# Second scores of the first group in shared PSUM banks, beside the next unit's first scores

## Chip, cores and metric

The kernel runs on one core of a Trainium2 chip. The metric is the device time of one execution in microseconds (us), as a median of several runs. The engines that matter are TensorE (PE in the profile, with its weight loads as PEld), VectorE (DVE), ScalarE (ACT), GpSimd (POOL) and SyncE (SP), which issues most transfers. They run their own instruction streams in order and wait for one another by semaphores.

## What is computed

A batch of 16 sequences of 100 tokens with 256 features goes through cross-attention on 361 context tokens (16 heads of 16 features), and then through a soft mixture of experts: 16 experts with 64 slots each. Both are residual.

```python
q, k, v = norm(x) @ wq + bq, ctx @ wk + bk, ctx @ wv + bv      # 16 heads of 16
alpha   = softmax(q k^T / 4 + mask)                            # over 361 keys
x       = x + (alpha v) @ wo + bo
xn      = layernorm(norm(x));  se = layernorm(slot_embeds) * scale
logits  = xn se^T                                              # 100 tokens, 1024 slots
slots   = softmax(logits over tokens)^T xn
eout    = (gelu(slots Wg + bg) * (slots Wu + bu)) Wd + bd      # per expert
x       = x + softmax(logits over slots) eout
```

Everything is in fp32.

## The kernel before

**Groups and units.** The 16 sequences are worked in groups of 2, 2, 4, 4 and 4 (`GROUPS`). A group's attention is cut into *units*: one sequence `b` and one block `cb` of four heads. The first group has 8 units. After a group's attention its logits and slots are made (`dispatch_quarter`), and then the stream of experts (`experts`, `down`, `combine_quarter`) runs over it, while units of the next group are laid between. Once the experts have begun there is always work for PE.

**A unit** (class `Unit`) has four steps:
- `maxima`: four products of 32 rows each (one per head, in the four 32-row strips of the array) put the *first scores*, tokens by keys, into the four PSUM banks of the tile `at` (L785); VectorE takes their negated maxima over the keys into `mxp` (L790).
- `queries`: PE transposes the maxima (L799, into a free corner of bank 0 of `at`), and VectorE adds them to the queries (L801), in a row that was kept free. The second scores so come out with the maximum taken off.
- `exponentials`: twelve products, three blocks of keys by four heads, put the *second scores*, keys by tokens, over the same four banks (L810); one ScalarE instruction takes the exponentials of all four, 121 by 1200 (L818).
- `values`: twelve products with the values (L833) give the unnormalised context and the sums; ScalarE copies them out (L842).

Since `at` serves both scores, a unit's first scores stand behind the exponentials of the unit before (`free_t`). The values of the last unit are taken after the first scores of the present one. Everything else on PE uses four further banks in turn (`mm_tile`).

**Beside the units** lie generators in the list `fill`: `key_work` (context transposes L584, keys L613, values L673, mask rows by DMA from SP L653), `query_work` (L519, L538), `parameter_work` (L405), `bo_work` (L423), `slot_work` (statistics of the slot embeddings L436, a power on GpSimd L447, their deviation L460, normalising them on ScalarE L467, transposing them L476 and L482) and `out_work` (reciprocal of the sums L713 and L714, output product L726, normalising the tokens L747, their transpose L752 and L758).

**What sets the order.** The kernel is written out in Python by a small planner: `Clock` keeps a modelled time for each engine and each bank, each generator yields the time at which its next step could go, how many banks it needs and the time that it needs on PE, VectorE and ScalarE, and the loop at the end takes the first task whose time has come. The modelled times only decide the order; on the chip the order stands and each instruction waits for what it needs. Until the experts begin (`begun`), a side task is only taken where it *fits* ahead of the next step of the unit, and where nothing fits the planner places a *warm* product: identity by identity, which nobody reads, into the last columns of bank 3 of `at` (L1344).

Of the kernel before, what the change touches and what calls it, by code (L numbers as in the profile page):

```python
# [33 lines left out]
F32 = mybir.dt.float32  # L34
AF = mybir.ActivationFunctionType
# [20 lines left out]
SLACK = 0.6  # L56
BACKLOG = 2.5
ASIDE = ("out_work", "query_work", "key_work")
MASK_DMA = 5.0
COLD = 7.0  # L60
HOP = 0.12
# [68 lines left out]
def xattn_ffn_kernel(  # L130
# [360 lines left out]
    def query_work(b, n=2):  # L491

        g = group_of[b]
        i0 = b - starts[g]
        yield x_t[g], 0, (0.0, 0.65 * n, 0.0)
        mv4 = two.tile([N, 2, 2], F32, tag="mv4", name="mv4")
        for i in range(n):
            ck.run("DVE", stats(accs[g][:, i0 + i, :], N, mv4[:, i, :]), x_t[g])
        r4 = rstd(mv4[:, :n, 1], N, n)
        t = ck.run("POOL", 0.7, ck.run("DVE", 0.15))  # L500
        yield t, 0, (0.0, 0.45 * n, 0.0)
        z4 = const.tile([N, 2, D], F32, tag="z4", name="z4")
# [24 lines left out]
        t = ck.copy(200 * n, ck.run("PE", 0.2 * n, t, ck.bank()))  # L527
        ck.free(t)
        yield t, 1, (0.7 * n, 0.5 * n, 0.5 * n)
        if b % 2 == 0:  # L530
            qp = two.tile([P, KD, 2, 2 * N], F32, tag="qp", name="qp")
        else:
            qp = qps[b - 1][0]
        cols = slice(b % 2 * N, (b % 2 + n) * N)
        ps = mm_tile("q_ps")
        for oc in range(KD):
            for kd in range(KD):
                nc.tensor.matmul(  # L538
                    ps[:, oc * n * N : (oc + 1) * n * N],
                    lhsT=w_sb["wq"][:, kd, oc * P : (oc + 1) * P],  # L540
                    rhs=xT[:, kd, : n * N],
                    start=kd == 0,
                    stop=kd == KD - 1,
                )
        t = max(ck.pe(400 * n, t, ck.bank()), par_t[0] if par_t[0] < NEVER else 10.5)
        for oc in range(KD):
            src = ps[:, oc * n * N : (oc + 1) * n * N]
            nc.vector.tensor_scalar(
                qp[:, oc, 0, cols], src, hm[:, 0:1], qb[:, oc, 0:1], ALU.mult, ALU.add
            )  # L550
            nc.scalar.activation(
                qp[:, oc, 1, cols], src, AF.Identity, bias=qb[:, oc, 1:2], scale=hm[:, 1:2]
            )
            first = ck.psum_dve(100 * n, t)
            t = ck.copy(100 * n, first)
            if b == oc == 0:
                qps[b] = (qp, first)
        ck.free(t)
        for i in range(n):
            qps.setdefault(b + i, (qp, t))  # L560
        yield (lambda: bo_t[0]), 0, (0.0, 0.0, 0.0)
        a = accs[g][:, i0 : i0 + n, :]
        nc.gpsimd.tensor_tensor(a, a, bo_bc[:N].unsqueeze(1).to_broadcast([N, n, D]), ALU.add)
        t = ck.run("POOL", 0.55 * n)
        for i in range(n):
            with_bo[b + i] = t
# [202 lines left out]
    class Unit:  # L769
# [10 lines left out]

        def maxima(self):

            for r in range(4):
                rows = slice(32 * r, 32 * r + 32)
                nc.tensor.matmul(  # L785
                    self.at[:N, r, :S2], lhsT=self.q[rows], rhs=self.k[rows], start=True, stop=True
                )
            m = MAXROW[self.par]
            mxv = mxps[self.par].rearrange("p (j c) -> p j c", c=32)
            nc.vector.tensor_reduce(  # L790
                mxv[:, :, m : m + 1], self.at[:N, :, :S2], AX.X, ALU.max, negate=True
            )
            self.t = ck.run("DVE", 1.66, ck.run("PE", 0.87, self.q_t, self.k_t, free_t[0]))
            phase[0] = "max"
# [10 lines left out]
        def exponentials(self):  # L805
# [15 lines left out]
            if self.cb == 3:  # L821
                live.discard(self.b)

        def values(self):
# [22 lines left out]
    free_t = [0.0]  # L847
    phase = [""]
    cx_t = {}
    group_of = {b: g for g, n in enumerate(GROUPS) for b in range(starts[g], starts[g] + n)}  # L850
# [6 lines left out]
    def values_ready(u):  # L857
        if u.b not in values_t or (u.cb == 0 and len(live_cxs) == 2):
            return NEVER
        return max(u.t, values_t[u.b])  # L860

    def units(g):
        last = None

# [6 lines left out]
                fill.append(Task(key_work(u.b + 2), ck))  # L871

        group = range(starts[g], starts[g] + GROUPS[g])
        for b in group:
            for cb in range(4):
                yield (
# [468 lines left out]

    def warm_up():

        warm_product()
        ck.pe(P)

    group = 0
    ck.t["DVE"], ck.t["ACT"], ck.t["POOL"] = 2.6, 4.6, 3.0
# [8 lines left out]
    while streams["experts"]:  # L1361
# [29 lines left out]
        if waiting:  # L1391
            units_first = dispatches[:WINDOW] + units_first
            side = sorted(fill, key=lambda t: t.kind != "out_work")
            if group == 1 and 0 in qps:
                kinds = (
                    "early_work",
                    "bo_work",
                    "query_work",
                    "parameter_work",
                    "slot_work",  # L1400
                    "out_work",
                    "key_work",
                )
# [18 lines left out]
        if not begun:  # L1422
# [3 lines left out]
            for i, t in enumerate(tasks):  # L1426
                if t is first_units:
                    lead = [i]
                    break
            else:  # L1430
                lead = [
                    i
                    for i, t in enumerate(tasks)
                    if t.kind in ("out_work", "all_experts") or t in dispatches[:1]
                ] if group > 1 else []
            soonest = min((ready[i] for i in lead), default=NEVER)
            by_keys = any(t.kind in ("key_work", "later_keys") and r <= now for t, r in zip(tasks, ready))
            for i, t in enumerate(tasks):
# [6 lines left out]
                late = 0.15 + SLACK * pe  # L1445
                if not first_units:
                    fits = max(end, vector, scalar) <= soonest + late
                elif phase[0] == "max":
                    fits = max(end, vector) <= soonest + late and scalar <= soonest + late + 1.2
                elif phase[0] != "queries":  # L1450
# [10 lines left out]
            if ready[-1] <= now:  # L1461
                ready[:-1] = [NEVER] * (len(ready) - 1)
        first = next((i for i, r in enumerate(ready) if r <= now), None)
        if first is None:
            first = min(range(len(ready)), key=lambda i: ready[i])
            assert ready[first] < NEVER
            if not begun and now + 0.2 < ready[first] and phase[0] != "queries":
                warm_up()
                continue
        task = tasks[first]  # L1470
        begun = begun or task is streams["experts"]
        task.step()
        if task.done:
# [63 lines left out]
```

## Time and profile before

| what | us |
|---|---|
| median of three runs (1175.8 to 1177.32) | 1176.27 |
| the profiled execution | 1176.62 |
| its span, first to last instruction | 1174.7 |
| TensorE busy | 1159.4 |
| VectorE, ScalarE, GpSimd busy | 632.8, 542.9, 153.6 |
| first scores of unit 0 start | 11.37 |
| values product of the last unit of the first group starts | 63.45 |
| first logits product | 72.64 |
| first expert product | 81.82 |

The granted TensorE clock is 0.999 of full speed. A row of an engine's order gives the start, the duration, the engine, the line, the operation, the tile written and those read, and after "x" the number of records; one fp32 product leaves two records on PE, a transpose one. In brackets stand the idle time ahead of it and what ended that. The ends of products are modelled, so that a group's length is best read from start to start.

### The profile page before, as it was taken

What the parts mean: (1) busy time and instruction counts of PE and PEld (TensorE: products, weight loads), DVE (VectorE), ACT (ScalarE), POOL (GpSimd) and SP (SyncE); (2) the same over time, 40 slices, a digit from 0 to 9 for tenths busy, and PEclk for the clock granted to TensorE, in tenths of its full rate; (3) what the DMA queues carried; (4) which work ended last, traced back from release to release, by engine and by line L of the source; (5) the groups of instructions that cost most, each with busy time, mean ns of one, the idle gap of its engine ahead of it and who ended that gap; (6) DMA issues with size and microseconds to landing.
All of it is one profiled execution on the core that took longest, in us unless ns stands there. A gap on an engine that the chain in (4) does not pass through costs nothing.

```text
span 1174.7 us, 24302 instructions
## 1 busy us (share of the span) xinstructions
PE 1159.4 (99%) x9825; PEld 899.3 (77%) x9825; DVE 632.8 (54%) x1561; ACT 542.9 (46%) x1112; POOL 153.6 (13%) x255
## 2 busy tenths in 40 slices
PE   8899999999999999999999999999999999999998
PEld 6587778778788777777777777787878878777876
DVE  5755545575644667644756655657533455432222
ACT  3557554655454765554435545446312336314110
POOL 3110301022000141400101000034000003002000
PEclk9999999999999999999999999999999999999999
DMA  4412656543467404232323213333344343345441
GB/s 134 137 38 99 233 174 203 163 148 114 139 213 233 115 20 86 78 113 95 83 80 108 95 38 113 113 126 112 113 155 145 113 149 127 112 132 161 138 131 55
DMA packets 138588, 144.85 MB, mean 123 GB/s; under 512 B 45050, under 2 KB 97228, under 8 KB 138476
## 3 DMA queue, kind: packets, MB, share of 16 engines
q1 hardware_dynamic: 137258, 141.50, 39.1%
q8 instruction: 78, 1.28, 0.5%
q0 software_dynamic: 496, 1.12, 0.3%
q10 hardware_dynamic: 722, 0.67, 0.2%
q14 instruction: 34, 0.28, 0.1%
HBM read 141.60 MB, written 1.66 MB: 122 GB/s over the span
## 4 chain that ended last, share of the span: by engine, by line
PE 97%; DVE 2%; ACT 1%; POOL 0%; issue 0%; DVEq 0%; POOLq 0%; ACTq 0%
PE gp L1291 20%; PE dn L1244 19%; PE up L1291 19%; PE sl L1032 5%; PE po L1162 5%; PE at L810 5%; PE at L785 4%; PE v_ps L673 4%; PE lg L942 4%; PE k_ps L613 3%; PE cx L833 3%; PE at L1344 1%; PE o_ps L726 1%; PE q_ps L538 1%; DVE mxp L790 1%; PE d_t L1020 1%
## 5 line engine op out<-in xcount | busy, mean ns | idle before, releaser
L1291 PE MATMUL gp<-ring,w_all 128*128 128x256 f32 (+1 forms) x1280 | 249.7, 341 | 1.8 <-ACT lg_all L963 1.3
L1291 PE MATMUL up<-ring,w_all 128*128 128x256 f32 (+1 forms) x1280 | 247.2, 339 | 0.0
L1307 DVE SCALAR_TENSOR_TENSOR hT<-up,parT,ge 128x256 f32<-128x256 f32 (+1 forms) x320 | 119.4, 423 | 224.6 <-PE up L1291 179.5
L1302 ACT ACTIVATE ge<-gp,parT 128x256 f32<-128x256 f32 (+1 forms) x320 | 116.9, 429 | 266.2 <-PE gp L1291 265.6
L1244 PE MATMUL dn<-w_all,hT 128*64 128x256 f32 x2048 | 232.5, 382 | 0.0
L1291 PEld LDWEIGHTS gp<-ring,w_all 128*128 128x128 f32 x1280 | 203.7, 191 | 30.1 <-issue 8.0
L1291 PEld LDWEIGHTS up<-ring,w_all 128*128 128x128 f32 x1280 | 205.0, 191 | 21.2 <-issue 0.8
L1244 PEld LDWEIGHTS dn<-w_all,hT 128*64 128x64 f32 x2048 | 142.4, 137 | 78.1 <-issue 8.9
L1253 DVE TENSOR_TENSOR ring<-dn,bd_bc 128x512 f32<-128x512 f32 x64 | 44.3, 692 | 144.0 <-PE dn L1244 143.9
L790 DVE TENSOR_REDUCE mxp<-at 100x4 f32<-100x1444 f32 x64 | 106.3, 1660 | 28.6 <-PE at L785 26.9
L818 ACT ACTIVATE aT<-at 121x1200 f32<-121x1200 f32 x64 | 74.9, 1170 | 49.3 <-PE at L810 45.0
L1302 ACT ACT_TABLE_LOAD x61 | 78.3, 1283 | 26.4 <-PE gp L1291 25.6
L1012 DVE STREAM_TRANSPOSE disp<-d_ex 32x128 f32<-32x128 f32 x256 | 77.3, 302 | 4.6
L717 POOL TENSOR_TENSOR cxs<-cxs,rs 128x100 f32<-128x100 f32 x63 | 24.9, 397 | 385.3 <-DVE rs L714 343.3
L1032 PE MATMUL sl<-disp,xn 100*128 100x256 f32 x256 | 63.0, 388 | 0.0
L997 POOL TENSOR_TENSOR d_ex<-d_ex,d_sm 128x400 f32<-128x400 f32 x28 | 23.7, 852 | 293.5 <-DVE d_sm L994 293.4
L1162 PE MATMUL po<-ring,lg_all 128*100 128x256 f32 x256 | 59.7, 382 | 0.1
L1047 ACT ACTIVATE ring<-sl,parT 128x256 f32<-128x256 f32 x64 | 32.6, 561 | 53.1 <-PE sl L1032 53.1
L810 PEld LDWEIGHTS at<-q,kT 32*121 32x121 f32 x1344 | 40.6, 180 | 19.8 <-issue 6.1
L818 ACT ACT_TABLE_LOAD x35 | 44.9, 1283 | 22.8 <-DVE q L801 12.5
L1032 PEld LDWEIGHTS sl<-disp,xn 100*128 100x128 f32 x256 | 46.6, 190 | 9.6 <-issue 2.8
L810 PE MATMUL at<-q,kT 32*121 32x100 f32 x1344 | 49.9, 277 | 3.6 <-DVE q L801 3.6
(152 smaller groups left out, 1273.0 us busy)
## 6 DMA issues: line engine op xcount, KB each, us to landing
w_all<-in_L_ffn_Wg_dram SPq DMA_DIRECT2D x80, 512.0 KB
w_all<-in_L_ffn_Wu_dram SPq DMA_DIRECT2D x80, 512.0 KB
w_all<-in_L_ffn_Wd_dram SPq DMA_DIRECT2D x80, 512.0 KB
bd_bc<-in_L_ffn_bd_dram SPq DMA_DIRECT2D x80, 64.0 KB
c_sb<-in_ctx_dram SPq DMA_DIRECT2D x96, 44.0 KB
acc<-in_x_dram SPq DMA_DIRECT2D x7, 200.0 KB
out_dram<-acc SPq DMA_DIRECT2D x7, 200.0 KB
ring<-n_L_ffn_slot_embeds_dram POOLq DMA_DIRECT2D x1, 1024.0 KB, 7.2
```

Source lines behind the costliest of these rows:

```text
L673: nc.tensor.matmul(ps[: KC + 1, :D], lhsT=cT[:, kd, c * KC : c * KC + KC + 1], rhs=w_sb["wv"][:, kd, :], start=kd == 0, stop=kd == KD - 1,)
L785: nc.tensor.matmul(self.at[:N, r, :S2], lhsT=self.q[rows], rhs=self.k[rows], start=True, stop=True)
L790: nc.vector.tensor_reduce(mxv[:, :, m : m + 1], self.at[:N, :, :S2], AX.X, ALU.max, negate=True)
L810: nc.tensor.matmul(self.at[: KC + 1, r, c * N : (c + 1) * N], lhsT=self.k[rows, c * KC : c * KC + KC + 1], rhs=self.q2[rows], start=True, ...
L818: nc.scalar.activation(self.aT[: KC + 1], self.at[: KC + 1, :, : 3 * N], AF.Exp)
L1012: nc.vector.transpose(dst[toks, :, :, a, :], src[32 * a : 32 * a + 32, :, :, toks])
L1032: nc.tensor.matmul(sl[:, kd * 256 : (kd + 1) * 256], lhsT=xns[g][:, b0 + i, kd * P : (kd + 1) * P], rhs=disp[:, i, :], start=True, stop=True,)
L1162: nc.tensor.matmul(pos[i][:N, :D], lhsT=lg_all[:, slot, 2 * c + i, :], rhs=eouts_of(g, q)[:, c, 2 * p + i, :], start=c == 0, stop=c == 1,)
L1244: nc.tensor.matmul(dn[S * x : S * x + S, i * D : (i + 1) * D], lhsT=hts[x][fc // FB][0].rearrange("p (f b s) -> p f b s", f=FB, s=S)[:, fc ...
L1291: nc.tensor.matmul(ps[:, f * T : (f + 1) * T], lhsT=w[:, kd, fc * P : (fc + 1) * P], rhs=slots_of(g, q)[:, j, kd].rearrange("p b s -> p (b ...
L1302: nc.scalar.activation(ge[:, cols], ps[:, cols], AF.Gelu, bias=col(8, e, fc))
L1307: nc.vector.scalar_tensor_tensor(out=hT[:, cols], in0=ps[:, cols], scalar=col(NPAR, e, fc), in1=ge[:, cols], op0=ALU.add, op1=ALU.mult,)
```

## The change

In the first group alone, a unit's second scores no longer go over the four banks of the first scores. They go into the common banks, in two halves of two heads (`half_exponentials`): two banks, six products and two exponentials of 300 columns each, and then the other two. Since the common banks are four, both halves fill them. The first scores are put into the banks of `at` in the order 1, 2, 3, 0, because the transpose of the maxima lies in bank 0.

The units of the first group are driven by a new generator, `first_units`: transpose and addition of the held unit, then the first scores of the next unit, then the values of the unit before, then the two halves of the held one.

Warm products that are placed after the first phase go into a common bank, if one is free, and not into `at`.

The planner's rules change with it. A budget `SPARE` (0.7) is set at each unit, and the steps of `slot_work`, `out_work`, `bo_work` and `parameter_work` may only be taken out of it; before the experts begin, a VectorE step of slots or output may go where VectorE is idle (`IDLE`); the order of preference among the side tasks is another one, with keys and queries first; `slot_work` counts among the leading tasks. In `query_work` the modelled time of the two copies is reckoned differently.

```diff
-            for r in range(4):
+            for r in (1, 2, 3, 0) if self.b < GROUPS[0] else range(4):
...
+        def half_exponentials(self, half):
+            if half == 0:
+                self.aT = two.tile([P, 4, 3 * N], F32, tag="aT", name="aT")
+                self.parts = []
+            ps = [mm_tile(f"sc{r}") for r in range(2)]
+            t = max(ck.bank(), ck.bank())
+            for c in range(3):
+                for r in range(2):
+                    rows = slice(32 * (2 * half + r), 32 * (2 * half + r) + 32)
+                    nc.tensor.matmul(
+                        ps[r][: KC + 1, c * N : (c + 1) * N],
+                        lhsT=self.k[rows, c * KC : c * KC + KC + 1],
+                        rhs=self.q2[rows],
+                        start=True,
+                        stop=True,
+                    )
+            tp = ck.run("PE", 0.55, self.t, t)
+            for r in range(2):
+                nc.scalar.activation(
+                    self.aT[: KC + 1, 2 * half + r], ps[r][: KC + 1, : 3 * N], AF.Exp
+                )
+                t = ck.act("exp", 290, tp)
+                ck.free(t)
...
+    def first_units(finish, group):
...
+        for n in nexts:
+            if held:
+                yield held.t, 0, (0.15, 0.25, 0.0)
+                held.queries()
+                phase[0] = "max"
+            if n and there(n):
+                yield from scores(n)
+            if before:
+                lt = before
+                yield (lambda: values_ready(lt)), 1, (0.7, 0.0, 0.3)
+                finish(before)
+                before = None
+            if held:
+                for half in range(2):
+                    yield held.t, 2, (0.5, 0.0, 0.9)
+                    held.half_exponentials(half)
+                before = held
...
     def warm_up():
-        warm_product()
-        ck.pe(P)
+        if not phase[0]:
+            warm_product()
+            ck.pe(P)
+            return True
+        if ck.bank_ready(1) > ck.t["PE"]:
+            return False
+        nc.tensor.matmul(mm_tile("warm")[:, :P], lhsT=ident, rhs=ident, start=True, stop=True)
+        ck.free(ck.pe(P, ck.bank()))
+        return True
...
                 kinds = (
+                    "key_work",
+                    "query_work",
+                    "bo_work",
+                    "parameter_work",
+                    "out_work",
+                    "slot_work",
                     "early_work",
-                    "bo_work",
-                    "query_work",
-                    "parameter_work",
-                    "slot_work",
-                    "out_work",
-                    "key_work",
                 )
...
+                elif t.kind in ("slot_work", "out_work", "bo_work", "parameter_work"):
+                    fits = ready[i] <= now and max(pe, dve, act) <= spare[0]
...
+        if not begun and ck.t["DVE"] <= now + IDLE:
+            for i, t in enumerate(tasks):
+                alone = t.needs[0] == 0 and t.needs[1] > 0
+                if alone and t.kind in ("slot_work", "out_work") and t.ready() <= now:
+                    first = i
+                    break
```

In the program as built the number of products is the same but for warm ones: 39 of them lie behind the first unit before, 25 after. The first expert product is preceded by 12 fewer value products, 6 fewer key products and 6 fewer context transposes than before.

More of the change, by code (lines that the diff above doesn't have):

```diff
@@ L58 @@
 ASIDE = ("out_work", "query_work", "key_work")
+SPARE = 0.7
+IDLE = 0.15
 MASK_DMA = 5.0
@@ L544, in query_work @@
                 )
-        t = max(ck.pe(400 * n, t, ck.bank()), par_t[0] if par_t[0] < NEVER else 10.5)
+        tm = max(ck.pe(400 * n, t, ck.bank()), par_t[0] if par_t[0] < NEVER else 10.5)
         for oc in range(KD):
@@ L553, in query_work @@
             )
-            first = ck.psum_dve(100 * n, t)
-            t = ck.copy(100 * n, first)
+            first = ck.psum_dve(100 * n, tm)
+            t = max(first, ck.copy(100 * n, tm))
             if b == oc == 0:
@@ L822, in exponentials @@
                 live.discard(self.b)
+        def half_exponentials(self, half):
[21 more added lines that the diff above has]
+                ck.free(t)
+            self.parts.append(t)
+            if half == 1:
+                self.t = t
+                if self.cb == 3:
+                    live.discard(self.b)
         def values(self):
@@ L847, in xattn_ffn_kernel @@
     free_t = [0.0]
+    spare = [0.0]
     phase = [""]
@@ L860, in values_ready, with there, scores @@
         return max(u.t, values_t[u.b])
+    def first_units(finish, group):
+        held = before = None
+        nexts = [(b, cb) for b in group for cb in range(4)] + [None, None]
+        def there(n):
+            b, cb = n
+            return (b, cb) in keys and b in qps
+        def scores(n):
+            b, cb = n
+            yield (
+                lambda: max(keys[b, cb][1], qps[b][1]) if there(n) else NEVER
+            ), 0, (0.0, 0.0, 0.0)
+            yield free_t[0], 0, (0.8, 1.7, 0.0)
+            u = Unit(b, cb)
+            u.maxima()
+            free_t[0] = u.t
+            spare[0] = SPARE
+            made.append(u)
+        made = []
+        for n in nexts:
[15 more added lines that the diff above has]
+                before = held
+            if n and not made:
+                if before:
+                    lt = before
+                    yield (lambda: values_ready(lt)), 1, (0.7, 0.0, 0.3)
+                    finish(before)
+                    before = None
+                yield from scores(n)
+            held = made.pop() if made else None
     def units(g):
@@ L873, in units @@
         group = range(starts[g], starts[g] + GROUPS[g])
+        if g == 0:
+            yield from first_units(finish, group)
+            return
         for b in group:
@@ L1433, in xattn_ffn_kernel @@
                     for i, t in enumerate(tasks)
-                    if t.kind in ("out_work", "all_experts") or t in dispatches[:1]
+                    if t.kind in ("out_work", "slot_work", "all_experts") or t in dispatches[:1]
                 ] if group > 1 else []
@@ L1466, in xattn_ffn_kernel @@
             assert ready[first] < NEVER
-            if not begun and now + 0.2 < ready[first] and phase[0] != "queries":
-                warm_up()
+            if not begun and now + 0.2 < ready[first] and phase[0] != "queries" and warm_up():
                 continue
         task = tasks[first]
+        if task.kind in ("slot_work", "out_work", "bo_work", "parameter_work"):
+            spare[0] -= max(task.needs)
         begun = begun or task is streams["experts"]
```

## The prediction

> **What bounds the kernel now.** I read the page's busy totals first, then busy time by stretch, then the TensorE order of the first group and beside it VectorE's and ScalarE's.
>
> The page's totals, and busy time by stretch (start:end, length, then busy us and instruction count of each engine, granted clock, DMA share, GB/s):
>
> ```profile
> PE 1159.4 (99%) x9825; PEld 899.3 (77%) x9825; DVE 632.8 (54%) x1561; ACT 542.9 (46%) x1112; POOL 153.6 (13%) x255
> ...
> 11.30:81.82 70.52, 64.24 (x702) 46.94 (x701) 45.56 (x107) 34.85 (x71) 13.00 (x31) 1.00 0.31 91
> 81.82:95.00 13.18, 11.84 (x89) 10.67 (x89) 6.51 (x15) 11.28 (x33) 0.00 (x0) 1.00 0.36 113
> 95.00:1174.70 1079.70, 1073.35 (x8987) 833.07 (x8984) 574.63 (x1409) 493.19 (x1003) 133.17 (x198) 1.00 0.41 125
> ```
>
> From 95 us on TensorE (PE) idles 6.35 us in all, most of it the drain after the last product. So whatever is done early, the rest is a fixed sum of PE work, and the end moves by: first expert product (81.82) earlier or later, plus PE work pushed behind it, plus new idle behind it. Before 81.82 there are 6.28 us of idle and the warm products of L1344: 78 records after 11.3 us, at 0.112 us each (22 of them from 73.99 to 76.45) 8.7 us.
>
> One unit of the first group, from the order of PE, then the VectorE and ScalarE rows of the same unit (start, duration):
>
> ```profile
> 24.64 0.87 PE L785 MATMUL at<-kT,qp 32*100 32x361 f32 x8
> ...
> 27.29 0.94 PE L1344 MATMUL at<-ident 128*128 128x128 f32 x6 [0.72 <-DVE mxp L790]
> 28.07 0.25 PE L799 MATMUL at<-ident,mxp 100*128 100x100 f32 x1
> 28.67 0.89 PE L810 MATMUL at<-q,kT 32*121 32x100 f32 x24 [0.35 <-DVE q L801]
> 29.49 1.48 PE L613 MATMUL k_ps<-cT,wk 128*128 128x361 f32 x4
> 30.91 0.87 PE L785 MATMUL at<-kT,qp 32*100 32x361 f32 x8
> ...
> 25.57 1.67 DVE L790 TENSOR_REDUCE mxp<-at 100x4 f32<-100x1444 f32 x1 [0.17 <-PE at L785]
> 28.35 0.26 DVE L801 TENSOR_TENSOR q<-at,qp 128x100 f32<-128x100 f32 x1 [0.98 <-PE at L799]
> ...
> 29.68 1.17 ACT L818 ACTIVATE aT<-at 121x1200 f32<-121x1200 f32 x1 [2.80 <-PE at L810]
> ```
>
> The reader sees a ring: first scores, maxima, transpose, addition, second scores, exponentials, and only then the next first scores, 6.27 us on. PE fills it with other work and with warm products, which hold the transpose up by about 0.8 us here.
>
> **The change, part by part.** *The ring is cut, but not all of it.* Second scores get their own banks, so the exponentials (second scores to next unit: 30.91 − 28.67 = 2.24 us) leave the ring. What the build shows: the next unit's first product waits for the addition (L801's successor), not just for the maxima, although bank 0 is filled last. So from first scores to first scores: 1.00 to the maxima (30.91 to 31.91), 1.66, 0.06, and 0.60 from transpose to the end of the addition = 3.32 us, with PE standing 0.5 us of it because the transpose is directly ahead of the next first scores.
>
> *Second scores cost more on PE.* Busy time of L810 alone, in three slivers of one unit (only the count of running PE records matters, in the first bracket):
>
> ```profile
> 14.71:14.86 0.15, 0.15 (x4) 0.15 (x8) 1.00 0.87 246
> 14.90:14.97 0.07, 0.07 (x8) 0.07 (x8) 1.00 0.72 293
> 15.00:15.02 0.02, 0.02 (x12) 0.02 (x8) 1.00 1.19 482
> ```
>
> Four records start together, one per 32-row strip; a round of four takes about 0.106 us, and 12 products x 2 records make six rounds, 0.82 us with fill and drain. Halves have two strips each: 12 rounds. Estimate: 0.64 for six more rounds, less a little overlap of fill: 1.40, so +0.58 per unit, +4.6 us over eight. [...] If the halves overlap fully it is 0.82. [...]
>
> *Exponentials.* Four of 300 columns: between the 100-column copy (0.24) and L818 (1.17 for 1200), 0.41 each; about 1.4 us from first to last against 1.17. ScalarE has the room; cover is PE's next unit, and without it 0.3 us a unit.
>
> *New waits by order.* VectorE now has things between maxima and addition: shuffle and reciprocal (0.26 + 0.78) in units 2, 3 and 6, a statistics pair (0.57) in 4 and 5. Behind the addition stand first scores of the next unit. In unit 7 it is statistics, then the slot deviation, whose power runs on GpSimd:
>
> ```profile
> 41.94 1.68 POOL L447 TENSOR_TENSOR rstd<-rstd,neghalf 128x8 f32<-128x8 f32 x1
> 43.65 0.17 DVE L460 SCALAR_TENSOR_TENSOR mv<-mv,rstd 128x8 f32<-128x8 f32 x1 [1.79 <-POOL rstd L447]
> ```
>
> and L460's successor, with the addition of unit 7 behind it. PE then waits 1.0 us for second scores 7.
>
> *The walk.* I put the build's order on the trace's durations (start-to-start on PE: first scores 0.80, values product 0.66, transpose 0.10, key product 1.34, value product 0.93, warm product 0.22). Same up to 14.03. First scores of unit 1 16.23, since two value products and the key transposes now precede it; unit 2 19.55; unit 3 23.50 (reciprocal ahead of the addition). Then two key products, six value products (all of batch 1) and the query product come before unit 4: 37.10, its maxima late by 0.5. Units 5, 6, 7: 41.10, 44.55, 48.55. Second scores 7 at 54.15, then a key product, and the last values product ends its slot at 57.55; before, 64.11 (63.45 + 0.66). PE idles 7.0 us in these units, in the order of the walk 0.3, 0.5, 1.0, 0.45, 0.3, 0.65, 0.5, 0.65, 1.05, 0.6 and 1.0.
>
> *The tail.* Slot normalisation and slot transposes, done between units before, now follow the last unit. ScalarE in order: key copy, copy of the last context (58.75), eight slot activations 4.1 (0.51 each), four slot copies 2.9, four token copies 1.5:
>
> ```profile
> 43.85 3.06 ACT L467 ACTIVATE ring<-ring,mv,rstd 128x256 f32<-128x256 f32 x6 [0.64 <-DVE mv L460]
> ...
> 50.41 1.43 ACT L482 ACTIVATE seT<-se_t,sgb 128x512 f32<-128x512 f32 x2
> ...
> 64.54 0.76 ACT L758 ACTIVATE xnT<-xn_t,parT 128x100 f32<-128x100 f32 x2
> ```
>
> So the first logits start at 67.0, against 72.64 before: 5.6 earlier, and with the same steps from there the first expert product at 76.2. What would have hidden the 7.0 us of slot activations, gaps between units, is gone; the tail's PE idles 3.0 us.
>
> *Work pushed behind it.* By the build's order 12 value products, 6 key products and 6 key transposes (batches 2 and 3) move behind the first expert product: 24 records of L673 5.6 (1.86 for 8), three pairs of L613 4.0, 0.7: 10.3 us.
>
> *Behind it.* Before, one stall of 1.34. Now the value product waits for the third logits copy (8.2 after the expert product, as before) and idles 1.9; the slot products wait for a copy queued on ScalarE behind a key activation, 1.0 more: 2.9, so +1.6. ScalarE is busy 11.28 of 13.18 us there already.
>
> *At nothing:* the planner's clock of the query step, SPARE and IDLE only move instructions, counted above. SP's queue: batch 3's mask rows go behind two weight loads, which wait for the first expert; the keys themselves are then only being made, so the cover is that lateness, and it would cost at most a stall of 2 us. Bias product and statistics lie beside the units.
>
> **Sum.** −5.6 + 10.3 + 1.6 = +6.3 us. Span 1174.7 + 6.3 = 1181.0; the profiled execution took 1176.62, 1.92 more than its span, and the median 1176.27 is 0.35 below it: 1182.6.
>
> **The rivals.**
> A, *half the loss* (14%): second scores stay at 0.82 and GpSimd's power takes the 0.54 of its one-column form. In the walk that saves 1.5 and 1.1: 1180.0. For it: row strips differ between halves. Against: records start in order.
> B, *faster* (6%): one mechanism, PE doesn't wait in first group and tail; it gains up to 7.0 + 3.0 + 1.6 = 11.6 us: 1171.0. It decides from 8.6 us on. For it: PE's own work fits; against: the wait for the addition is in the program.
> C, *no difference* (10%): the cut ring just pays for halves and tail, 1176.3: about half of B's gain, for example if value products fill the stall behind the expert product and tail copies overlap.
> D, *worse* (10%): ScalarE's stretch behind the first expert product slips further, with new stalls of 4 to 5 us: 1187.
> The forecast itself holds 60%.
>
> **How the numbers follow.** A measurement here tells 0.2% (2.35 us) from nothing. Faster: B and an edge of C, 0.07. Same: most of C and an edge of A, 0.11. Slower: the forecast, A, D, 0.82. The unknown costs (0.82 to 1.64 for scores, 0.54 to 1.68 for the power, tail waits) give the forecast its own 1179 to 1186; with A, D and part of C the range is 1176 to 1187.5.
>
> **What the profile would show.** Ring: first scores of units 1 to 2 about 3.3 us apart, 5 to 6 3.4, with a PE gap of 0.5 after each transpose, ended by the addition. Halves: from first record to next work 1.4. Last values product at 57.6; logits 67; first expert product 76. PE idle between that product and 95 about 2.9. Wrong if the last values product ends before 52 (waits smaller), or if the logits follow it by less than 7 us (the tail isn't ScalarE's), or if idle shows up after 100 us.

## The result and the profile after

The changed kernel takes 1194.57 us (median of 4 runs, 1193.4 to 1196.71) against 1176.43 before: 1.0151 times as long, 95% interval 1.0138 to 1.0163. The forecast was 1182.6, range 1176 to 1187.5: right in direction, but the loss is 18.1 us instead of 6.3.

The profiled execution took 1195.29 us, with a span of 1193.5. From its page, the busy totals and two rows of the 40 slices:

```profile
PE 1173.2 (98%) x9797; PEld 909.8 (76%) x9797; DVE 631.5 (53%) x1559; ACT 547.2 (46%) x1140; POOL 150.9 (13%) x255
...
PE   9989999999999999999999999999999999999998
...
PEclk9789999999999999999999999999999999999999
```

TensorE has 28 records fewer and is busy 13.8 us longer. The third row shows where to look: in the second and third slice (30 to 90 us) the granted clock is 0.7 and 0.8, where the kernel before shows 9 in every slice and a mean of 0.999. Busy time by stretch, in the stretches of the prediction and in two more (start:end, length, busy us and records of PE, PEld, DVE, ACT, POOL, granted clock, DMA share, GB/s):

```profile
11.30:84.59 73.29, 66.43 (x632) 49.24 (x631) 40.91 (x100) 32.86 (x89) 13.10 (x31) 0.82 0.28 84
84.59:95.00 10.41, 8.44 (x53) 6.67 (x52) 4.00 (x10) 8.90 (x28) 0.00 (x0) 0.98 0.01 2
95.00:1193.50 1098.50, 1088.39 (x9062) 844.96 (x9062) 580.33 (x1419) 502.13 (x1019) 130.41 (x198) 1.00 0.41 124
16.54:44.06 27.52, 24.54 (x316) 17.70 (x315) 19.24 (x44) 12.00 (x35) 1.57 (x4) 1.00 0.41 130
44.06:64.55 20.49, 19.89 (x197) 13.62 (x198) 9.63 (x26) 6.52 (x20) 3.57 (x5) 0.50 0.15 39
78.20:85.03 6.83, 6.75 (x20) 5.96 (x20) 1.46 (x4) 1.51 (x4) 0.00 (x0) 0.50 0.00 0
```

From unit 6 to behind the last unit, and again in the tail (from the first logits to the first expert product), TensorE ran at half its clock: 27.3 us in all. PE is busy 97% of the first of these stretches and does no more for it: 197 records in 20.49 us, where the kernel with nothing pushed behind the experts, at full clock, left 237 from 44.06 to 64.55. At full clock the unit goes as the prediction walked it. PE's order, units 2 and 3 (start, duration):

```profile
19.86 0.87 PE L788 MATMUL at<-kT,qp 32*100 32x361 f32 x8 [0.35 <-DVE q L804]
20.65 0.72 PE L866 MATMUL cx<-aT,vpad 120*32 120x100 f32 x24
21.31 1.30 PE L837 MATMUL sc<-q,kT 32*121 32x100 f32 x24
22.54 0.30 PE L802 MATMUL at<-ident,mxp 100*128 100x100 f32 x1
23.62 0.87 PE L788 MATMUL at<-kT,qp 32*100 32x361 f32 x8 [0.78 <-DVE q L804]
```

The second scores take 1.23 (21.31 to 22.54; forecast 1.40, before 0.82), and the stand behind the transpose is 0.35, or 0.78 where VectorE has shuffle and reciprocal between. Unit 6 in the half-clock stretch has the same rows, with other lengths:

```profile
44.28 1.54 PE L788 MATMUL at<-kT,qp 32*100 32x361 f32 x8 [0.39 <-DVE q L804]
45.75 1.23 PE L866 MATMUL cx<-aT,vpad 120*32 120x100 f32 x24
46.91 2.07 PE L837 MATMUL sc<-q,kT 32*121 32x100 f32 x24
48.91 0.43 PE L802 MATMUL at<-ident,mxp 100*128 100x100 f32 x1
49.69 1.54 PE L788 MATMUL at<-kT,qp 32*100 32x361 f32 x8 [0.35 <-DVE q L804]
```

The loss on PE, term by term, from the two profiled executions (the gaps in PE's order are added up for idle time, and a gap that crosses 95 us counts ahead of it; pushed work goes by the time to the next start):

| term | forecast | measured |
|---|---|---|
| first expert product | −5.6 (76.2) | +2.8 (84.59) |
| key and value work pushed behind it | +10.3 | +10.3 (5.58 + 4.07 + 0.63) |
| idle behind it, to 95 us | +1.6 | +1.15 (2.49, before 1.34) |
| idle from 95 us on | 0 | +3.3 (5.83, before 2.51) |
| all other products behind it | 0 | +1.4 |
| drain behind the last product | 0 | −0.1 (3.77, before 3.89) |
| sum, the difference of the spans | +6.3 | +18.8 |

### The profile page after: what moved, and what is told of

The parts are those of the page before. It is cut to its first block, busy times and chain, and to the rows that moved or that the text cites. A ratio compares the mean times of both kernels' runs of the same rounds, so it can differ in the third digit from the quotient of the medians.

```text
span 1193.5 us, 24271 instructions
## 1 busy us (share of the span) xinstructions
PE 1173.2 (98%) x9797; PEld 909.8 (76%) x9797; DVE 631.5 (53%) x1559; ACT 547.2 (46%) x1140; POOL 150.9 (13%) x255
## 4 chain that ended last, share of the span: by engine, by line
PE 93%; DVE 2%; DMA 2%; ACT 1%; SPq 0%; issue 0%; ACTq 0%; POOL 0%; DVEq 0%; POOLq 0%
PE dn L1331 19%; PE gp L1378 19%; PE up L1378 18%; PE sl L1119 5%; PE po L1249 5%; PE at L788 4%; PE at L813 4%; PE lg L1029 4%; PE cx L866 4%; PE v_ps L675 3%; PE k_ps L615 3%; DMA w_all<-in_L_ffn_Wd_dram 2%; PE o_ps L728 1%; DVE mxp L793 1%; PE sc L837 1%; PE q_ps L540 1%
## 5 line engine op out<-in xcount | busy, mean ns | idle before, releaser
L821 ACT ACTIVATE aT<-at 121x1200 f32<-121x1200 f32 x56 | 65.6, 1172 | 33.7 <-PE at L813 32.7
L788 PE MATMUL at<-kT,qp 32*100 32x361 f32 x448 | 49.9, 515 | 3.8 <-DVE q L804 2.2
L875 ACT COPY cxs<-cx 128x100 f32<-128x100 f32 x64 | 15.5, 242 | 79.3 <-PE cx L866 78.0
```

Of the source, the lines that this page charges most:

```text
L788: nc.tensor.matmul(self.at[:N, r, :S2], lhsT=self.q[rows], rhs=self.k[rows], start=True, stop=True)
L821: nc.scalar.activation(self.aT[: KC + 1], self.at[: KC + 1, :, : 3 * N], AF.Exp)
```

## The experiments

Two theories at first. *T*: most of what the forecast lacks is the clock; the array had too little work in the units to keep it. *W*: the time goes into waits and pushed work, and the clock only coincides. "Half" below is the half-clock time ahead of 104 us in the profiled execution (three kernels have 3.4 us more between 210 and 420 us: units alone, rules alone, and the two together), "mean clock" that of each execution.

**More warm products in the changed kernel**

```diff
             nc.tensor.transpose(tp, mxps[self.par], ident[:N, :N])
+            if self.b < GROUPS[0]:
+                for _ in range(3):
+                    warm_product()
```

> The changed kernel with three more warm products (identity by identity, unread) behind each transpose of the maxima in the first group, 24 in all; the order of all else is the same. Theory T: about 10 us of the loss come from the granted TensorE clock, which was 0.50 from 44.06 to 64.55 us and from 78.2 to 85.03 because the array had too little work in the units. Then the clock stays at 1.00 in the units, the first expert product comes at 78 to 79.5 instead of 84.59, and the time falls to 1187 to 1189 (the second halving, behind the wait for the dispatch weights, may stay). Theory W: the time goes into waits and pushed work, and the half clock only coincides with them. Then 24 products of 0.22 us, 5.3, fill gaps of 3.5 us and the time is 1194 to 1197.

1189.73 us, 1.0101 of before (1.0086 to 1.0116): 24 more products make the kernel about 5 us faster. Half fell from 27.3 to 6.8 us, and the first expert product came at 80.37. It is a little slower than T said; 3.4 us of half clock stayed in the units (48.2 to 51.6). One of its four executions had a mean clock of 1.000 and took 1187.62. Its tail, at full clock, took 9.08 us instead of the changed kernel's 12.14. W is out as an account of the whole loss.

**The same products on a small part of the array**

```diff
+            if self.b < GROUPS[0]:
+                for _ in range(3):
+                    nc.tensor.matmul(at_all[:32, 3, 384:],
+                        lhsT=ident[:32, :32], rhs=ident[:32], start=True, stop=True)
```

> As the changed kernel with three more warm products behind each transpose in the first group, but each over 32 rows and 32 columns of the array (a block of 32 by 32 of the identity with 32 rows of it) instead of 128 by 128, with the same 128 elements streamed, so the same time on TensorE. T1, the clock is held by time in which TensorE is busy, whatever part of the array works: as with full products, mean clock 0.997 or more, time 1187 to 1191. T2, it is held by the part of the array that works: the clock halves as in the changed kernel, mean clock 0.988 to 0.992, 1194 to 1199.

1200.6 us, 1.0188 (1.0148 to 1.0227). The two kernels in the stretch from first scores 4 to the last record of the last values products, first with full and then with small products, have the same number of records:

```profile
39.53:62.35 22.82, 20.08 (x276) 14.71 (x276) 13.88 (x32) 7.64 (x23) 3.18 (x4) 0.93 0.48 142
```

```profile
40.12:70.61 30.49, 28.54 (x276) 19.23 (x276) 14.35 (x33) 7.70 (x24) 3.17 (x4) 0.63 0.34 108
```

And the groups of these products, from 16 to 60 us, full and small (of 48 records each; the slower kernel has more of its behind 60 us):

```profile
L1434 PE MATMUL at<-ident 128*128 128x128 f32 x42 | 6.0, 279 | 0.0
```

```profile
L805 PE MATMUL at<-ident 32*32 32x128 f32 x36 | 6.0, 308 | 0.0
```

Between products that fill PE's time about equally and differ in the part of the array that works, the clock is mostly kept or mostly lost: half is 6.8 us with the one and 30.7 with the other. That is T2 and not T1, though the loss goes beyond T2's range, and one of the four executions all but kept the clock. The small products use fewer rows and fewer columns and load smaller weights; which of these counts was not separated. The run also shows the price within one program: its four executions had mean clocks 0.998, 0.987, 0.987 and 0.982, and took 1190.32, 1200.47, 1200.72 and 1204.39 us.

**The kernel before without its later warm products**

```diff
     def warm_up():
-        warm_product()
+        if not phase[0]:
+            warm_product()
         ck.pe(P)
```

> The kernel before, with the 39 warm products that lie behind the first unit left out; all else in the same order. T: the gaps stand empty, the array has too little work in the units, the granted clock halves there in some stretches of 6.8 us or more, and the time rises to 1181 to 1190. W: the warm products hold transposes up by some tenths of a us a unit (about 0.8 in one), so the time falls to 1170 to 1176 and the clock stays at 1.00.

1176.07 us, 0.9994 (0.9985 to 1.0003): neither range. The clock did halve, for 3.4 us in the units and 6.8 in the tail; but the logits started at 70.43 instead of 72.64, since the warm products had held transposes up (by 0.78 us in the unit of the prediction, 27.29 to 28.07). In the tail the same steps then took 12.23 us instead of 9.18. So both theories' effects are there: 2.2 us gained, 3.05 lost to 6.8 us of half clock.

**Units alone, rules alone.** First the new units with the planner's rules of before, then the old units with the new rules (there the warm products go back into `at` too):

```diff
-                elif t.kind in ("slot_work", "out_work", "bo_work", "parameter_work"):
-                    fits = ready[i] <= now and max(pe, dve, act) <= spare[0]
...
-        if not begun and ck.t["DVE"] <= now + IDLE:
...
-                    if t.kind in ("out_work", "slot_work", "all_experts") or t in dispatches[:1]
+                    if t.kind in ("out_work", "all_experts") or t in dispatches[:1]
```

> The changed kernel's units (cut ring, halves) with the planner's rules of before (order of the side tasks, no budget, no idle rule, slot work not leading). Ahead of the first expert product stand six value products and two key products more than in the changed kernel, so 2.7 us less is pushed behind it, and 49 warm products instead of 25. T: the clock stays at 1.00 in the units because of the warm products, and the time is 1180 to 1187. W, with the loss in the units themselves: 1190 to 1196, whatever the clock.

```diff
-        if g == 0:
-            yield from first_units(finish, group)
-            return
...
-            for r in (1, 2, 3, 0) if self.b < GROUPS[0] else range(4):
+            for r in range(4):
```

> The units of before (second scores over the banks of the first, twelve products and one exponential) with the changed planner's rules. All key and value products stand ahead of the first expert product, as before, and four query products more. T: if 19 warm products behind the first unit are too few, the clock halves in the units and the time is 1180 to 1190; if it holds, 1174 to 1179. W, with the loss in the rules (slot and output work put off): 1182 to 1190 at a clock of 1.00. If the loss is all in the new units: 1174 to 1178.

In these two texts I had miscounted: 26 warm products stand in the first behind the first unit, not 49, and 35 in the second, not 19; and what is pushed back in the first is 4.1 us less, not 2.7. Measured: 1190.74 (1.011, 1.0095 to 1.0125; half 17.1) and 1185.59 (1.0057, 1.0035 to 1.008; half 13.7). Each alone is slower than before, and each loses the clock, so the loss does not come from one of the two parts only. With the old units one execution had mean clock 0.999 and took 1181.8: some 5 us are lost there almost without it.

**No halves**

```diff
-                for half in range(2):
-                    yield held.t, 2, (0.5, 0.0, 0.9)
-                    held.half_exponentials(half)
+                yield held.t, 4, (0.85, 0.0, 1.7)
+                held.all_exponentials()
```

`all_exponentials` writes the twelve products, strip after strip, to four common banks.

> The changed kernel with all second scores of a unit in one step: twelve products over the four strips into the four common banks, and four exponentials. The halves cost 1.23 us on TensorE from start to start where the clock was full, against 0.82 before: 0.4 a unit, 3.3 us. Two key, six value products and three context transposes more stand ahead of the first expert product. Theory T (the clock): TensorE has still less to do in the units, so the clock halves again, for 7 us or more, and the time is 1186 to 1193. Theory H (the halves are what costs): 3.3 us and what depends on them come back, 1180 to 1187 with the first expert product at 81 or earlier.

1184.87 us, 1.0056 (1.004 to 1.0071); first expert product at 81.33, half 3.4 us. So H's number came out, but not H's reason alone: the planner put 4.8 us less work behind the expert product (two key products, six value products and six transposes less), and the clock held in the units, against what T expected. How much of the 9.7 us is the halves can't be read from this run.

**Transposed maxima in a common bank**

```diff
-            tp = self.at[:, 0, 512 - N :]
+            tp = mm_tile("mx_t")[:, :N] if g0 else self.at[:, 0, 512 - N :]
```

> The changed kernel with the transposed maxima in a common bank, so that the next unit's first scores wait for the maxima of the unit before and not for its addition. In the changed kernel TensorE stands 0.35 to 0.4 us before five of the first scores. T: less standing, but the clock is what costs: 1188 to 1195, clock halved for 10 us or more. Theory W (waits in the ring): 2 to 3 us less than the changed kernel, 1191 to 1193, whatever the clock does.

1191.5 us, 1.0122 (1.0104 to 1.014). First scores 1 to 2 are 2.95 us apart instead of 3.32, so the wait for the addition is gone. Half is 13.7 us, and the times go by the mean clock here too (0.994 at 1189.95 to 1192.41, 0.989 at 1196.2). The number fits both.

**Nothing pushed behind the experts**

```diff
-            units_first = dispatches[:WINDOW] + units_first
+            units_first = (dispatches[:WINDOW] if begun or 3 in values_t else []) + units_first
```

> The changed kernel with logits and slots held back until the values of batch 3 are made, so that all key and value products of the first two groups stand ahead of the first expert product, as before. 10.3 us are then no longer behind it. Theory T: behind the first expert product 1089 to 1090 us are left as before, with 3.9 us of idle time instead of 8.3; ahead of it the 10.3 us lie partly in waits of the tail and the clock halves for 10 to 20 us, so the expert product comes at 90 to 94 and the time is 1182 to 1187. Rival P (pushing the work back gained nothing and lost nothing): the expert product comes at 95 and the time is 1187 to 1195.

1184.8 us, 1.0051 (1.0035 to 1.0067), with mean clocks 1.000, 0.997, 0.995 and 0.992 at 1180.42, 1183.99, 1185.61 and 1185.6. The profiled one is the first, with full clock throughout: expert product at 86.83, earlier than T said, since it had reckoned with half clock; 1088.0 us behind it on PE and 4.6 idle. Until behind the last unit PE's order is the same as in the changed kernel, so this is the changed kernel's group at full clock. Units 6 and 7:

```profile
43.99 0.87 PE L788 MATMUL at<-kT,qp 32*100 32x361 f32 x8 [0.39 <-DVE q L804]
44.79 0.72 PE L866 MATMUL cx<-aT,vpad 120*32 120x100 f32 x24
45.44 1.30 PE L837 MATMUL sc<-q,kT 32*121 32x100 f32 x24
46.68 0.30 PE L802 MATMUL at<-ident,mxp 100*128 100x100 f32 x1
47.76 0.87 PE L788 MATMUL at<-kT,qp 32*100 32x361 f32 x8 [0.78 <-DVE q L804]
```

The last unit's values products start at 56.15, in the changed kernel at 62.03; the walk of the prediction had them at 56.9 (its slot's end at 57.55 less 0.66). The whole half-clock stretch is measured from first scores 6 to the warm product that is the first to start behind it in the changed kernel: 13.78 us here (43.99 to 57.77), 20.53 there (44.28 to 64.81). So 20.5 us at half clock cost 6.75 us.

**The two together, and all three**

First the kernel without halves and with nothing pushed behind the experts; then also with the maxima in a common bank and the tail's warm products in `at`:

> The changed kernel without halves (twelve second-score products over four strips, four common banks) and with logits held back until the values of batch 3 are made: what is left is the cut ring and the planner's rules, with no work pushed behind the first expert product. With halves and the clock at 1.00 that product came at 86.8 us, with 1088 us behind it. Halves off takes 3.3: 83.5, PE's end at 1171.5, and the time 1177 where the clock holds, up to 1182 where it halves for up to 10 us. Rival (the halves cost nothing, since PE waits there anyway): 1180 where the clock holds, up to 1185.

> As the one before, and with the transposed maxima in a common bank and warm products of the tail in the bank of the first scores. First scores then wait for the maxima alone (ring 2.9 to 3.0 instead of 3.3 us), which gains 0.35 us a unit where nothing else stands there. T: the clock holds in the tail; the first expert product comes at 81 to 83, the time is 1174.5 to 1178. Rival: the gaps move to the next wait, and it is within 1 us of the one before.

1185.32 us (1.0074, 1.006 to 1.0087; half 6.8, in the tail) and 1185.84 (1.0075, 1.0059 to 1.009; half 10.2, in the units). The rival of the first was nearer: first scores come no earlier than with halves (unit 4 at 37.57 against 36.84, unit 7 at 49.55 against 47.76), PE is idle 9.4 us ahead of the experts instead of 8.6, and what the shorter second scores save goes into waits and warm products. So taking the halves out gained nothing in this order, though they cost PE 0.4 us a unit; the planner also moved other work, so their own worth is not shown. The second kernel came out as its rival said, and above T: its tail kept the clock, as T had it (9.16 us), but the units lost it.

**One part of the change alone.** The kernel before, with the warm products of the changed kernel; then with those of the tail back in `at`:

```diff
     def warm_up():
-        warm_product()
-        ck.pe(P)
+        if not phase[0]:                  # second kernel: if not phase[0] or group > 1:
+            warm_product()
+            ck.pe(P)
+            return True
+        if ck.bank_ready(1) > ck.t["PE"]:
+            return False
+        nc.tensor.matmul(mm_tile("warm")[:, :P], lhsT=ident, rhs=ident, start=True, stop=True)
+        ck.free(ck.pe(P, ck.bank()))
+        return True
```

> The kernel before with one part of the change alone: warm products behind the first unit go into a common bank where one is free, not behind the maxima into the bank of the first scores. 23 of them stand behind the first unit instead of 39. Without any, the logits started at 70.4 instead of 72.6 us, but the clock then halved for 6.8 us in the tail and the first expert product came at 82.7 instead of 81.8. T: with warm products that stand in the waits instead of behind them the clock holds and those 2 us stay: 1172.5 to 1175. Rival: 23 are too few, the clock halves in some stretch, and the time is 1175.5 to 1178.

> The kernel before with warm products in a common bank while the units run (13 of them), and in the bank of the first scores in the tail behind the last unit (25), where no first scores are near. In the run with the common bank everywhere the logits started at 69.2 us, then the clock halved for 6.8 us in the tail, and the first expert product came at 81.4, 12.2 behind the logits instead of 9.2. T: the clock holds in the tail, the expert product comes at 78.5 to 79.5, and the time is 1171 to 1173.5. Rival (12.2 us are the steps of the tail and not the clock): the expert product stays at 81 to 81.5 and the time is 1174 to 1176.

1174.32 us, 0.9976 (0.9967 to 0.9985), and 1173.43 us, 0.9971 (0.9959 to 0.9982). Both are faster than the kernel before, by 0.2 to 0.3%, and so than the changed one. Of the first, seven of 11 executions came out as T said (mean clock 0.998 or 0.999, 1173.41 to 1174.78 us) and four as the rival said, the profiled one among them (0.997, 1175.94 to 1176.35); the second came out as T said. A unit of the second kernel, to be set beside that of the prediction:

```profile
25.50 0.94 PE L1355 MATMUL warm<-ident 128*128 128x128 f32 x6
26.29 0.30 PE L799 MATMUL at<-ident,mxp 100*128 100x100 f32 x1
26.95 0.89 PE L810 MATMUL at<-q,kT 32*121 32x100 f32 x24 [0.35 <-DVE q L801]
```

The warm products no longer wait for the maxima (0.72 us before); they fill that wait. The tail from first logits to first expert product, in the first and in the second of the two:

```profile
69.17:81.39 12.22, 9.71 (x41) 8.67 (x40) 3.50 (x9) 4.25 (x15) 2.23 (x4) 0.73 0.01 1
```

```profile
69.37:78.55 9.18, 9.17 (x66) 8.70 (x65) 3.51 (x9) 4.35 (x15) 2.24 (x4) 1.00 0.01 2
```

With the same real work, the second has 25 more records of warm products in the wait and keeps the clock, and its expert product comes 2.8 us earlier.

## Why the prediction was right and wrong

**What failed: "I put the build's order on the trace's durations".** Those durations were of full clock, and the walk kept them to the end: a loss of clock stood at nothing, and without a reason. Until 44 us that held (forecast and measured first scores: 16.23 and 16.54, 19.55 and 19.86, 23.50 and 23.62, 37.10 and 37.12, 41.10 and 40.93, 44.55 and 44.28); then the clock halved. Of the 8.4 us by which the first expert product missed 76.2, 5.1 lie ahead of the last values products (62.03, forecast 56.9), 0.3 between them and the logits, and 2.95 in the steps from the logits on (12.14 us instead of 9.18). The same order at full clock puts the price of the clock at 6.75 us from unit 6 on; the two kernels with one part alone, and the changed kernel with more warm products (9.08), show it for the tail. Together that is 9.7 us, so the rest of the walk came out 1.3 us shorter than forecast. The wait in the tail, in the kernel before and then in the changed one:

```profile
73.99 2.62 PE L1344 MATMUL at<-ident 128*128 128x128 f32 x22
76.45 0.51 PE L519 MATMUL x_t<-ident,z 100*128 100x100 f32 x4
```

```profile
73.87 0.83 PE L1442 MATMUL warm<-ident 128*128 128x128 f32 x6
77.06 0.62 PE L1107 MATMUL d_t<-ident,d_ex 128*100 128x128 f32 x4 [2.36 <-DVE d_ex L1084]
...
78.35 3.78 PE L1119 MATMUL sl<-disp,xn 100*128 100x256 f32 x8
81.92 2.88 PE L1029 MATMUL lg<-xnT,seT 128*128 128x200 f32 x8
84.59 2.16 PE L1378 MATMUL gp<-ring,w_all 128*128 128x128 f32 x16
```

Before, 22 warm records stood in that wait; the change leaves 6, because it wants a free common bank. What stands ahead of the prediction counts the warm products that go (39 to 25); the prediction has them only as 8.7 us of PE time, and not as what keeps the clock.

**"From 95 us on the rest is a fixed sum" was wrong by 4.7 us.** The pushed work itself was right: 24 more records of L675 and 12 of L615 stand behind the first expert product (groups from 84.59 on, and the same of before from 81.82):

```profile
L675 PE MATMUL v_ps<-wv,cT 128*121 128x256 f32 x168 | 41.7, 385 | 1.8 <-ACT lg_all L1050 1.7
L615 PE MATMUL k_ps<-cT,wk 128*128 128x361 f32 x108 | 36.7, 474 | 1.0 <-DVE cT L601 1.0
```

```profile
L673 PE MATMUL v_ps<-wv,cT 128*121 128x256 f32 x144 | 35.5, 385 | 0.1
L613 PE MATMUL k_ps<-cT,wk 128*128 128x361 f32 x96 | 33.2, 475 | 0.0
```

But the stream that starts with other work goes on in another order, with new stalls late in it. Between 195 and 280 us:

```profile
L1331 PE MATMUL dn<-w_all,hT 128*64 128x256 f32 x96 | 12.2, 383 | 1.4 <-DMA w_all<-in_L_ffn_Wd_dram 1.4
L615 PE MATMUL k_ps<-cT,wk 128*128 128x361 f32 x20 | 6.6, 470 | 1.0 <-DVE cT L601 1.0
```

The longest stall behind 100 us comes further on. The kernel with nothing pushed behind the experts (second line) has it as well:

```profile
432.56 0.87 PE L788 MATMUL at<-kT,qp 32*100 32x361 f32 x8 [1.56 <-ACT aT L821]
417.69 0.87 PE L788 MATMUL at<-kT,qp 32*100 32x361 f32 x8 [1.55 <-ACT aT L821]
```

So pushing alone does not explain the late stalls. In the kernels that have the new units or the new rules, idle time from 100 us on is 3.7 to 6.6 us where work is pushed and 2.6 to 4.6 where none is, against 2.5 before: new orders have new stalls, and which order makes which stall was not tried. The 1.4 us by which other products take longer stay open too, but for the 0.2 of them that is the end of the half-clock stretch (84.59 to 85.03).

**Right.** The ring: 3.32 us from unit 1 to 2, as forecast, set by the addition; moving the maxima to another bank took that wait away (2.95). Stands behind the transpose 0.35 to 0.39, forecast 0.5. ScalarE's chain in the tail: 4.04 us of slot activations and 2.89 of slot copies, forecast 4.1 and 2.9. Idle up to 95 us: 2.49, forecast 2.9.

**Sizes off.** Second scores: 1.23 instead of 1.40. No run shows 1.64, twice 0.82, the upper end that the forecast allows for them: at full clock the halves took 1.23 and 1.24 from start to start (21.31 to 22.54, and 45.44 to 46.68 in the kernel with nothing pushed), 1.5 times the 0.82 of before. The stand ahead of second scores 7 was 0.58 at full clock, forecast 1.0.

**The rivals.** A needed second scores at 0.82 us and GpSimd's power at 0.54; they took 1.23 and 1.68. B and C needed shorter waits, and PE idled no less than before between 11.3 us and the first expert product (6.9 us, and 8.6 in the kernel with nothing pushed; before 6.3). D put new stalls on ScalarE's stretch behind the first expert product; that stretch idled less than forecast, and the new stalls came later. None of them, nor the range, had the clock in it. The forecast named idle time behind 100 us as a sign of error, and it came (5.83 us, before 2.50). With full clock the changed kernel would have taken about 1185 us (an estimate: 1194.57 less 9.7), inside the range; the execution with 24 more warm products and a mean clock of 1.000 took 1187.62. So the clock is what put the forecast out; the late stalls and slower products, 4.7 us, were partly made up by the 1.3 us above and the shorter idle time ahead of 95 us.

## What to carry to other kernels

A product that nobody reads may be there for the clock: before you take it out, or place smaller products closer together, weigh how much of the array works in each stretch of a few us, not only whether TensorE is busy. Here the same number of products left 6.8 us at half clock over the whole array and 30.7 over 32 rows and 32 columns. Put such products into a bank that nobody waits for: then they fill a wait instead of making one (0.9976 of the time before, in the kernel before with that alone). When work moves from an early stage into a stream that is full, count it there in full (10.3 us here, as forecast); and when an early stage is reordered, look for new stalls late in the stream (5.83 us idle from 95 us on, before 2.51).

## What was unexpected in the hardware

The clock halved with no gap of more than 0.86 us on PE in the units, and with PE busy 61% of the 3.4 us ahead of it. The half-clock stretches lasted 20.48 and 6.83 us in the changed kernel, and 10.24 and 3.41 in the one with the transposed maxima in a common bank: six, two, three and one times 3.413. What sets these lengths was not shown.

The records can be read in stretches of that length. Below is the one ahead of the halving in the changed kernel, and one of the kernel before that kept its clock:

```profile
40.65:44.06 3.41, 2.10 (x33) 1.53 (x33) 2.39 (x6) 1.36 (x4) 0.00 (x0) 1.00 1.02 341
40.14:43.55 3.41, 2.17 (x34) 1.68 (x34) 1.62 (x5) 1.98 (x3) 3.01 (x3) 1.00 1.09 355
```

PE is busy 61% and 64%, with as many records; but the second has full warm products among them. Count as work each product's rows times columns times elements streamed, against 128-by-128 products back to back (0.112 us for 128 elements): by that estimate from the rows the array did 31% in the first and about 39% in the second. In the changed kernel the stretch from 91.84 to 95.26 us kept the clock with PE busy 56%, less than the 61% ahead of the halving; the estimate gives it 39%. Another kept it with PE busy 76% and an estimated 35% (16.75 to 20.17). The stretch ahead of the halving in the tail, 74.78 to 78.19, had PE busy 33%. At half clock a busy PE was not enough to get the clock back: from 50.88 to 57.71 us PE was busy throughout and the clock stayed at half; from 61.12 to 64.54 it was busy throughout too, and the clock behind it was full. Apart from the small products above, no experiment tested this reading, and where the clock turns was not measured.

From execution to execution the mean clock of one kernel differs: 0.982 to 0.998 with the small products, 0.992 to 1.000 with nothing pushed behind the experts, and 0.998 to 1.000 in the kernel before. Each us at half clock cost about 0.33 us in the units (6.75 for 20.5) and 0.45 in the tail (3.05 for 6.8). That it is less than half goes with two things that the rows show for the units: from start to start the products took less than twice as long (first scores 1.47 instead of 0.80, second scores 2.00 instead of 1.24), and from 44.06 to 64.55 us PE idled 0.60 us, where the kernel at full clock, with nothing pushed, idled 2.31. What each of the two makes up was not measured.
